# A short scan's preparation put into other steps, a convolution moved between its parts, and its drive made by GpSimd

## The chip, the cores and the metric

The kernel runs on one core of a Trainium2 chip. The metric is the device time of one execution, in microseconds. The program is one launch, and most of its instructions stand in an order that the kernel itself writes out, engine by engine.

## The reference

The input is a batch of 8 images, 64 x 64 positions of 96 channels, float32. Two layers follow each other, and each adds its result to its input:

```python
x = x + layer0(group_norm(x))
x = x + layer1(group_norm(x))
```

A layer projects 96 channels to 2 x 192 (`xp` and `z`), runs a depthwise 3x3 convolution and SiLU over `xp`, scans the result in four directions (rows, columns, and both backwards), adds the four, normalizes over channels, multiplies with silu(z) and projects back to 96. The scan of layer 0 has 16 states per channel:

```python
delta = softplus(dt @ dt_proj + bias)
h = exp(delta * A) * h + delta * B * u      # per position, 16 states
y = sum(h * C) + u * D
```

The scan of layer 1 is written with cumulative sums:

```python
dt = softplus(dt @ dt_proj_w + dt_proj_b)
decay = exp(cumsum(dt * A))
h = decay * cumsum(dt * B * u / (decay + 1e-12))
y = sum(h * C) + u * D_skip
```

Because of the term 1e-12, `h` dies away once the decay has fallen far enough, so only the beginning of each direction needs a scan at all. The kernel scans the first 160, 40, 24 and 16 positions of each direction for the four groups of four states (a constant of the kernel, with a general path for other data).

## The kernel before

Channels lie on partitions in two halves (`h`) of 96. A scan works on *sets*: 32 channels times 4 states fill 128 partitions, and a set has 1024 positions. Four sets (index `i`, 0 to 3) make a *group* of 32 channels, three groups (`g`) a *job*, which is one half of one *unit*. An image has 16 units of layer 0 (4 directions, 4 stretches), so 32 jobs and 384 sets. From the second image on, one short unit follows at the end: layer 1's scan of the image before, with 2 jobs of 3 sets of 128 x 960, 6 sets in all. Seven of the eight images have one.

The loop in `scan_rows` runs over the sets with a step number n, and each engine executes what it is given in the order of the calls. With `at(i)` as the set n + i, one step holds, in this order:

- `fetch`: SP issues the loads that spread dt and delta * u over 128 partitions (`dt_rep`, `dtu_rep`, two buffers each; for short sets also `cum_rep`). It is 5 steps ahead for ordinary groups and 2 for short sets. `replicate` and `replicate_short` load B and C (`b_rep`, `c_rep`).
- `advance_set(at(0))`: VectorE multiplies `drive` (in PSUM) with B (L895) and scans (L908). For short sets it multiplies with the gate in between (L898) and runs two scans (L903).
- `keep_state` (L919): ScalarE copies the last column, except in a direction's last stretch.
- `fill(at(1))`: ScalarE's exponential writes the decay to PSUM (L861, for short sets four pieces, L857). The pool `pslot` has two buffers.
- `drive(at(2))`, for short sets `drive(at(1))`: ScalarE copies delta * u to PSUM (L878), once a group.
- `release(at(-4))`: after a group's last set, ScalarE copies the four quarters of its sum out of PSUM (L990); for short sets `y_short` (L980).
- `gate(at(1))`: ScalarE's Tanh for a short set, four pieces (L872).
- `read_out(at(-1))`: GpSimd multiplies the scan with C (L924).
- `early(at(2))`: in the last set of a group (i = 3), GpSimd makes delta * u * B from SBUF in place of VectorE (L885), so this set has no L895.
- `collect(at(-3))`: TensorE sums over states into `acc` (L960, short sets L937). At i = 0 it first brings in what was there (L951). The pool of `acc` has one buffer.
- then the stages that stand in `plan` for this step.

Job m begins at step 12m - 1; with that as s = 0 the steps of a job are counted below. A group's `release` and the next group's first `collect` fall on s = 0, 4 and 8. In each job the stages prepare job m + 2: `ready` for an ordinary one, `short_ready` for a short one. The latter's stages are `argument` (TensorE, dt's projection), `parts`, `exponential`, `logarithm`, `rounded`, `rounding` (ScalarE: Relu and Abs, Exp, Ln, and the rounding error of 1 + exp), `total` (TensorE adds four terms, L760), `delta` (ScalarE copies the sum out, L769), `again` (TensorE, L778) and `running` (VectorE's running sum of dt, L787), `extend` (six copies on ScalarE, L505), `lowest` (eight small ScalarE instructions and two on VectorE), `product` (GpSimd, dt * u, L772) and `store` (seven memsets on GpSimd, then three DMAs on SP to DRAM). The logarithm needs its own table: ScalarE loads it and then loads the exponential's again.

All these matmuls and the convolution share one PSUM buffer (`pmisc`, tag "mm"). The convolutions for later images run beside the scan, one window a job (`conv_beside`, `windows`): 9 taps in 3 or 4 steps on TensorE (L1027), then one step for the Tanh on ScalarE (`curve`, L1037), then `product` on VectorE (L1040) and a store. Stages of the convolution stand in `plan` before those of the preparation in the same step. Jobs 30 and 31 prepare the short unit. Images 1 to 6 (counted from 0) have a convolution window in both; image 7 has none there.

Of the kernel before, what the change touches and what calls it, by code (L numbers as in the profile page):

```python
# [8 lines left out]
F32 = mybir.dt.float32  # L9
# [11 lines left out]
T = 1024  # L21
# [3 lines left out]
P = 128  # L25
# [4 lines left out]
NS = N // GS  # L30
# [23 lines left out]
def two_ss2d_layers(ctx: ExitStack, tc: tile.TileContext, t: dict, out: bass.AP):  # L54
# [368 lines left out]
    def scan_rows(xc, y, parts, plan, rows, beside):  # L423

        with (
            tc.tile_pool(name="loads", bufs=2, side="right") as loads,
            tc.tile_pool(name="piece", bufs=1) as piece,
            tc.tile_pool(name="work", bufs=2) as work,
            tc.tile_pool(name="pslot", bufs=2, space=PSUM) as pslot,
            tc.tile_pool(name="pdrive", bufs=1, space=PSUM) as pdrive,
            tc.tile_pool(name="pacc", bufs=1, space=PSUM) as pacc,  # L440
            tc.tile_pool(name="pmisc", bufs=1, space=PSUM) as pmisc,
        ):
            units, jobs, sets, x_dbl = parts
            total = len(sets)
            plan = plan(pmisc)
            with tc.manual_schedule():
                state = None
                plan.setdefault(-1, []).insert(0, lambda: low_rows(x_dbl, units[1], rows))
                for n in range(-AHEAD, max(total + 4, max(plan, default=0) + 1)):
                    at = lambda i: sets[n + i] if 0 <= n + i < total else None  # L450
                    m, j = divmod(n + 1, PER)
                    if j == 0 and 0 <= m < len(jobs):

                        stages = []
                        if m + 2 < len(jobs):
                            prepare = short_ready if jobs[m + 2]["unit"]["short"] else ready
                            stages += prepare(xc, x_dbl, jobs[m + 2], piece, pmisc)
                        if m % NH == 1 and m // NH + 2 < len(units):
                            unit = units[m // NH + 2]
                            project = short_projection if unit["short"] else projection  # L460
                            stages += project(xc, x_dbl, unit, rows, pmisc)
                        for step, stage in stages:
                            plan.setdefault(n + step, []).append(stage)
                    fetch(at(AHEAD), False, loads)
                    fetch(at(2), True, loads)
                    replicate(at(AHEAD_BC), x_dbl, loads)
                    replicate_short(at(AHEAD_BC), "b", loads)
                    replicate_short(at(AHEAD_BC - 1), "c", loads)
                    if at(0) and at(0)["unit"]["nth"] == 0 and at(0)["first"]:
                        state = piece.tile([P, D // GC * NS], F32, name="state0", bufs=2)  # L470
                    advance_set(at(0), state, work)
                    keep_state(at(-1))
                    fill(at(1), pslot)
                    drive(at(2), False, pdrive)
                    drive(at(1), True, pdrive)
                    release(at(-4), y, beside)
                    gate(at(1))
                    read_out(at(-1), work)
                    early(at(2), work)
                    collect(at(-3), xc, y, pacc)  # L480
                    for stage in plan.pop(n, []):
                        stage()
                assert not plan
# [235 lines left out]
    def short_ready(xc, x_dbl, job, piece, pmisc):  # L719
# [48 lines left out]
        def delta(s):  # L768
            nc.scalar.copy(job["ln"][:, halves[s]], job["v"])  # L769
# [17 lines left out]
            nc.vector.tensor_tensor_scan(out, ones_reset, src, 0.0, ALU.mult, ALU.add)  # L787

        def lowest():
            extend(job["cum"])  # L790
            last = small.tile([C, NS * K], F32, name="last_short")
            for i in range(NS):
                for d in range(2):
                    a, b = place(i, 2 * d), place(i, 2 * d + 1)
                    at = slice(a.start, b.start + 1, HEADS[i])
                    if d == 0:
                        at = slice(a.stop - 1, b.stop, HEADS[i])
                    nc.scalar.activation(
                        last[:, K * i + 2 * d :][:, :2],
                        job["cum"][:, at],  # L800
                        AF.Copy,
                        scale=w["least1"][:, h, i : i + 1],
                    )
            low = small.tile([C, 1], F32, name="lowest_short")
            nc.vector.tensor_reduce(low, last, mybir.AxisListType.X, ALU.min)
            nc.vector.tensor_tensor(worst, worst, low, ALU.min)

        def store():

            for i in range(NS):  # L810
                for j in (OFFSETS[i], OFFSETS[i] + HEADS[i]):
                    if j > 0:
                        nc.gpsimd.memset(job["ln"][:, j : j + BLOCK : BLOCK - 1], 1e30)
            job["dt"] = job["ln"]
            for c in ("dt", "dtu", "cum"):
                job[f"{c}_far"] = dram.tile([C, HT], F32, name=f"{c}_short", bufs=3)
                nc.sync.dma_start(job[f"{c}_far"], job[c])

# [3 lines left out]
            (1, lambda: argument(1)),  # L822
            (2, lambda: parts(1)),
            (3, exponential),
            (4, logarithm),
            (4, rounded),
            (5, rounding),
            (6, lambda: total(0)),
            (7, lambda: delta(0)),
            (7, lambda: total(1)),  # L830
            (8, lambda: delta(1)),
            (8, lambda: running(1)),
            (8, lambda: again(0)),
            (9, product),
            (9, lambda: running(0)),
            (10, lowest),
            (11, store),
        ]

    def column(s):  # L840
# [2 lines left out]

    def by_gpsimd(s):

        return s["i"] == NS - 1

    def fill(s, pslot):

# [21 lines left out]
                cum = blocks(s["group"]["cum"], i)  # L871
                nc.scalar.activation(cum, cum, AF.Tanh, bias=half_log, scale=rate)  # L872

    def drive(s, short, pdrive):

        if s and s["i"] == 0 and s["unit"]["short"] == short:
            s["group"]["drive"] = pdrive.tile([P, T], F32, name="drive")[:, : s["unit"]["n"]]
            nc.scalar.copy(s["group"]["drive"], s["group"]["dtu"])  # L878

    def early(s, work):  # L880

        if s and by_gpsimd(s):
            s["buf"] = work.tile([P, T], F32, name="set", bufs=SETS)[:, : s["unit"]["n"]]
            b = s["unit"]["b", s["i"]]
            nc.gpsimd.tensor_tensor(s["buf"], s["group"]["dtu"], b, ALU.mult)  # L885
# [202 lines left out]
    def windows(first, n, b):  # L1088
# [3 lines left out]
        for m in range(first, first + n):  # L1092
# [2 lines left out]
            projects = m % NH == 1 and (unit < K // 2 * NT or b >= 1 and unit == K * NT)  # L1095
            assert m < last
            if b >= 1 and m + NH >= K * NT * NH:
                found.append((at + 10, (3, 3, 3), 1))
            elif projects:
                found.append((at + 5, (3, 3, 3), 1))  # L1100
            else:
                found.append((at + 3, (3, 2, 2, 2), 2))
# [886 lines left out]
```

## Time and profile before

| | |
|---|---|
| time, median of 3 runs | 12404.24 us (12389.48 to 12425.54) |
| profiled execution | 12404.1 us, its span 12402.2 us |
| VectorE (DVE) busy | 10960.4 us, 88% |
| GpSimd (POOL) busy | 10508.3 us, 85% |
| ScalarE (ACT) busy | 9688.3 us, 78% |
| TensorE (PE) busy | 9540.3 us, 77% |
| mean DMA rate | 149 GB/s |
| L878, drive copy, 128x1024 | 997 ns |
| L885, delta * u * B on GpSimd, 128x1024 | 2357 ns mean |
| L924, times C on GpSimd, 128x1024 | 2359 ns mean |
| L898, gate of a short set on VectorE | 1157 to 2262 ns |

In the lines of a profile, a row of a group gives its busy time and the mean of one instruction, then the idle time of its engine just ahead of it and what ended that. In a timeline a row gives the start, the length, the engine and the line, and in brackets the idle time before it with the instruction that ended it; "x4" means that four instructions were merged. In a table of windows the columns are the length, the busy times of TensorE, its weight loads, VectorE, ScalarE and GpSimd, the granted TensorE clock, the share of the DMA engines and GB/s.

### The profile page before, as it was taken

What the parts mean: (1) busy time and instruction counts of PE and PEld (TensorE: products, weight loads), DVE (VectorE), ACT (ScalarE), POOL (GpSimd) and SP (SyncE); (2) the same over time, 40 slices, a digit from 0 to 9 for tenths busy, and PEclk for the clock granted to TensorE, in tenths of its full rate; (3) what the DMA queues carried; (4) which work ended last, traced back from release to release, by engine and by line L of the source; (5) the groups of instructions that cost most, each with busy time, mean ns of one, the idle gap of its engine ahead of it and who ended that gap; (6) DMA issues with size and microseconds to landing.
All of it is one profiled execution on the core that took longest, in us unless ns stands there. A gap on an engine that the chain in (4) does not pass through costs nothing. (4 is left out here: it accounts for less than half of the span.)

```text
span 12402.2 us, 134216 instructions
## 1 busy us (share of the span) xinstructions
PE 9540.3 (77%) x44312; PEld 3022.4 (24%) x44312; DVE 10960.4 (88%) x6870; ACT 9688.3 (78%) x15131; POOL 10508.3 (85%) x4802
## 2 busy tenths in 40 slices
PE   5875578787888778877788777888788887886565
PEld 1221122222222222222222222222222222222122
DVE  6999889996999969999799987999879998899976
ACT  4888778887887868878788787887778877788874
POOL 3999889996999969998699986999879987799974
PEclk8887778888888878888888878887788877887786
DMA  3444344444444444444444454444544445444430
GB/s 96 165 155 156 127 159 161 154 156 152 148 164 160 161 138 164 163 162 147 148 156 158 162 165 135 160 162 161 163 138 153 156 156 158 136 165 160 157 123 23
DMA packets 666561, 1853.80 MB, mean 149 GB/s; under 512 B 184936, under 2 KB 199150, under 8 KB 665757
## 3 DMA queue, kind: packets, MB, share of 16 engines
q1 hardware_dynamic: 658685, 1832.52, 44.6%
q10 hardware_dynamic: 7168, 12.59, 0.3%
q8 instruction: 352, 5.77, 0.2%
q14 instruction: 356, 2.92, 0.1%
HBM read 1533.82 MB, written 311.02 MB: 149 GB/s over the span
## 5 line engine op out<-in xcount | busy, mean ns | idle before, releaser
L924 POOL TENSOR_TENSOR out<-set,c_rep 128x1024 f32<-128x1024 f32 x3114 | 7290.0, 2359 | 884.4 <-PE acc L960 317.8
L908 DVE TENSOR_TENSOR_SCAN set<-decay,state,set 128x1024 f32<-128x1024 f32 x2304 | 5366.3, 2345 | 407.4 <-ACT decay L861 189.6
L861 ACT ACTIVATE decay<-dt_rep,w_a 128x1024 f32<-128x1024 f32 x3072 | 3420.2, 1114 | 335.7 <-DVE set L908 329.8
L895 DVE TENSOR_TENSOR set<-drive,b_rep 128x1024 f32<-128x1024 f32 x2346 | 2811.1, 1198 | 43.1 <-DMA b_rep<-x_dblr 28.2
L1027 PE MATMUL ps_conv<-edged,taps 96*96 96x512 f32 (+1 forms) x4032 | 2476.3, 754 | 54.5 <-DVE dt L787 25.9
L960 PE MATMUL acc<-out,w_gather 128*32 128x256 f32 x24576 | 2274.2, 480 | 8.1 <-POOL out L924 7.7
L908 DVE TENSOR_TENSOR_SCAN set<-decay,set 128x1024 f32<-128x1024 f32 x768 | 1744.4, 2286 | 224.5 <-ACT decay L861 146.6
L885 POOL TENSOR_TENSOR set<-dtu_rep,b_rep 128x1024 f32<-128x1024 f32 x768 | 1810.1, 2357 | 93.9 <-DMA b_rep<-x_dblr 51.6
L951 PE MATMUL acc<-map,w_eye 96*32 96x256 f32 x4608 | 568.5, 575 | 1483.4 <-ACT map L990 1253.5
L990 ACT COPY map<-acc 32x256 f32<-32x256 f32 x3072 | 1470.5, 479 | 45.8 <-PE acc L960 5.6
L960 PEld LDWEIGHTS acc<-out,w_gather 128*32 128x32 f32 x24576 | 781.8, 130 | 1939.5 <-issue 1282.0
L1027 PEld LDWEIGHTS ps_conv<-edged,taps 96*96 96x96 f32 (+1 forms) x4032 | 727.5, 200 | 1405.4 <-issue 1244.3
L919 ACT COPY state<-set 128x1 f32<-128x1 f32 x2304 | 426.1, 185 | 754.3 <-DVE set L908 747.9
L634 PE MATMUL ps_sp<-z,w_eye 96*96 96x512 f32 x960 | 658.2, 774 | 288.8 <-ACT ln L643 244.4
L655 POOL TENSOR_TENSOR dtu<-ln,map 96x1024 f32<-96x1024 f32 x256 | 670.7, 2620 | 237.2 <-DVE ln L651 133.0
L878 ACT COPY drive<-dtu_rep 128x1024 f32<-128x1024 f32 (+1 forms) x810 | 808.0, 997 | 34.7 <-DMA dtu_rep<-dtu_far 30.1
L602 PE MATMUL ps_dt<-x_dbl,w_dtw 7*96 7x512 f32 x1024 | 595.4, 663 | 301.2 <-ACT z L615 151.0
L951 PEld LDWEIGHTS acc<-map,w_eye 96*32 96x32 f32 x4608 | 101.4, 121 | 1954.6 <-ACT map L990 1656.1
L634 PE MATMUL ps_sp<-dtu,w_eye 96*96 96x512 f32 x960 | 554.6, 662 | 0.0
L634 PE MATMUL ps_sp<-ln,w_eye 96*96 96x512 f32 x960 | 535.5, 642 | 0.0
L614 ACT ACTIVATE dt<-ps_dt 96x512 f32<-96x512 f32 x512 | 303.0, 592 | 279.2 <-PE ps_dt L602 260.0
L634 PE MATMUL ps_sp<-dt,w_eye 96*96 96x512 f32 x960 | 506.7, 610 | 0.0
(239 smaller groups left out, 9496.8 us busy)
## 6 DMA issues: line engine op xcount, KB each, us to landing
dt_rep<-dt_far SPq DMA_DIRECT2D x768, 512.0 KB
dtu_rep<-dtu_far SPq DMA_DIRECT2D x768, 512.0 KB
b_rep<-x_dblr SPq DMA_DIRECT2D x256, 512.0 KB
c_rep<-x_dblr SPq DMA_DIRECT2D x256, 512.0 KB
b_rep<-x_dblc SPq DMA_DIRECT2D x256, 512.0 KB
c_rep<-x_dblc SPq DMA_DIRECT2D x256, 512.0 KB
dt_far<-ln SPq DMA_DIRECT2D x256, 384.0 KB
dtu_far<-dtu SPq DMA_DIRECT2D x256, 384.0 KB
```

Source lines behind the costliest of these rows:

```text
L634: nc.tensor.matmul(job["ps"][:C, :], w["eye"], job[term][:, halves[s]], start=i == 0, stop=i == 3,)
L655: nc.gpsimd.tensor_tensor(like(job["dtu"], col), like(job["dt"], col), positions(xc[:, h, :], col, t0, T), ALU.mult,)
L861: nc.scalar.activation(s["decay"], s["group"]["dt"], AF.Exp, scale=rate)
L878: nc.scalar.copy(s["group"]["drive"], s["group"]["dtu"])
L885: nc.gpsimd.tensor_tensor(s["buf"], s["group"]["dtu"], b, ALU.mult)
L895: nc.vector.tensor_tensor(s["buf"], s["group"]["drive"], b, ALU.mult)
L908: nc.vector.tensor_tensor_scan(ordered(s["buf"], unit), ordered(s["decay"], unit), ordered(s["buf"], unit), 0.0 if unit["nth"] == 0 else s ...
L924: nc.gpsimd.tensor_tensor(s["out"], s["buf"], s["unit"]["c", s["i"]], ALU.mult)
L951: nc.tensor.matmul(acc, lhs[:, GC * g : GC * (g + 1)], positions(old[:, h, :], unit["column"], unit["t0"] + at, n), start=True, stop=False ...
L960: nc.tensor.matmul(acc, w["gather"], s["out"][:, at : at + n], start=False, stop=s["i"] == NS - 1, skip_group_check=True,)
L990: nc.scalar.copy(yk, like(acc, unit["column"]))
L1027: nc.tensor.matmul(job["ps"][:C, :], taps[l][:k, h, tap, :], edged[:k, tap // 3 : tap // 3 + rows, tap % 3 : tap % 3 + WW], start=tap == 0 ...
```

## The change

`short_ready` keeps `argument`, `parts` and `exponential` at s = 0 to 3. `rounded` moves from 4 to 5, `logarithm` from 4 to 6, the two `total` from 6 and 7 to 8 and 9, the two `delta` from 7 and 8 to 9 and 10, `running` and `again` from 8 and 9 to 10 and 11, `product` from 9 to 11. `extend` is taken out of `lowest` and stands at 11 behind `running(0)`; `store` moves from 11 to 12, with the running sum stored first; `lowest` moves from 10 to 13. For the second short job 13 is the step of the first short set. The convolution's windows in jobs 30 and 31 begin at s = 3 in place of s = 10, so their nine taps stand at 3, 4, 5, the curve at 6, the product at 7.

For short sets, GpSimd makes delta * u * B (`by_gpsimd` is true), one step ahead and after `read_out`; the copy to PSUM and VectorE's product are left out for them.

```diff
-                    drive(at(2), False, pdrive)
-                    drive(at(1), True, pdrive)
+                    drive(at(2), pdrive)
                     release(at(-4), y, beside)
                     gate(at(1))
                     read_out(at(-1), work)
-                    early(at(2), work)
+                    early(at(2), False, work)
+                    early(at(1), True, work)
...
         def lowest():
-            extend(job["cum"])
...
-            for c in ("dt", "dtu", "cum"):
+            for c in ("cum", "dt", "dtu"):
...
             (3, exponential),
-            (4, logarithm),
-            (4, rounded),
+            (5, rounded),
             (5, rounding),
-            (6, lambda: total(0)),
-            (7, lambda: delta(0)),
-            (7, lambda: total(1)),
-            (8, lambda: delta(1)),
-            (8, lambda: running(1)),
-            (8, lambda: again(0)),
-            (9, product),
-            (9, lambda: running(0)),
-            (10, lowest),
-            (11, store),
+            (6, logarithm),
+            (8, lambda: total(0)),
+            (9, lambda: delta(0)),
+            (9, lambda: total(1)),
+            (10, lambda: delta(1)),
+            (10, lambda: running(1)),
+            (10, lambda: again(0)),
+            (11, product),
+            (11, lambda: running(0)),
+            (11, lambda: extend(job["cum"])),
+            (12, store),
+            (13, lowest),
         ]
...
     def by_gpsimd(s):
-        return s["i"] == NS - 1
+        return s["unit"]["short"] or s["i"] == NS - 1
...
-    def drive(s, short, pdrive):
-        if s and s["i"] == 0 and s["unit"]["short"] == short:
-            s["group"]["drive"] = pdrive.tile([P, T], F32, name="drive")[:, : s["unit"]["n"]]
+    def drive(s, pdrive):
+        if s and s["i"] == 0 and not s["unit"]["short"]:
+            s["group"]["drive"] = pdrive.tile([P, T], F32, name="drive")
             nc.scalar.copy(s["group"]["drive"], s["group"]["dtu"])
-    def early(s, work):
-        if s and by_gpsimd(s):
+    def early(s, short, work):
+        if s and by_gpsimd(s) and s["unit"]["short"] == short:
...
             if b >= 1 and m + NH >= K * NT * NH:
-                found.append((at + 10, (3, 3, 3), 1))
+                found.append((at + 3, (3, 3, 3), 1))
```

## The prediction

> **What bounds the kernel now.** First the page's busy times and costliest groups.
>
> ```profile
> PE 9540.3 (77%) x44312; PEld 3022.4 (24%) x44312; DVE 10960.4 (88%) x6870; ACT 9688.3 (78%) x15131; POOL 10508.3 (85%) x4802
> L924 POOL TENSOR_TENSOR out<-set,c_rep 128x1024 f32<-128x1024 f32 x3114 | 7290.0, 2359 | 884.4 <-PE acc L960 317.8
> L908 DVE TENSOR_TENSOR_SCAN set<-decay,state,set 128x1024 f32<-128x1024 f32 x2304 | 5366.3, 2345 | 407.4 <-ACT decay L861 189.6
> ```
>
> VectorE sets the pace: three sets in four cost it a product and a scan, 3.56 us from scan end to scan end in the timeline, the fourth a scan alone, 2.3. Where it idles it mostly waits for ScalarE's decays (L861). ScalarE can't run far ahead: `pslot` has two buffers, so the decay of set s+1 starts when scan s-1 has ended. That leaves it 3.56 us a step for 1.1 us of decay and all else.
>
> Then the stretch that the change touches: two jobs of 12 sets (from the end of scan 359 to the end of scan 383), by the windows view, the last four columns being ScalarE, GpSimd, clock and DMA.
>
> ```profile
> 4307.13:4402.06 94.93, 67.57 (x317) 20.42 (x315) 80.71 (x51) 71.02 (x112) 77.80 (x49) 0.77 0.53 157
> 5816.07:5914.87 98.80, 72.20 (x319) 22.13 (x317) 80.73 (x52) 70.64 (x112) 77.93 (x49) 0.74 0.52 150
> 7324.75:7422.77 98.02, 70.59 (x319) 21.64 (x317) 80.71 (x51) 70.59 (x112) 77.86 (x49) 0.75 0.51 151
> 8832.49:8929.78 97.29, 69.67 (x318) 21.46 (x316) 80.82 (x51) 70.75 (x112) 77.90 (x49) 0.75 0.52 152
> 11845.46:11936.85 91.39, 48.12 (x286) 14.97 (x284) 80.01 (x50) 69.64 (x110) 77.83 (x48) 0.72 0.39 128
> ```
>
> These are images 2 to 5 and 7 (7 has no convolution there). With images 1 and 6 (93.6 and 94.9, each lacking one scan's record, so 3.5 longer) the mean of 1 to 6 is 97.4, of which VectorE idles 16.7. VectorE's timeline of image 1 tells on what:
>
> ```profile
> 2820.95 2.35 DVE L908 TENSOR_TENSOR_SCAN set<-decay,state,set 128x1024 f32<-128x1024 f32 x1 [1.95 <-ACT decay L861]
> 2830.96 0.82 DVE L787 TENSOR_TENSOR_SCAN dt<-ones_reset,ps_sp 96x320 f32<-96x320 f32 x1 [1.85 <-ACT ln L769]
> 2855.06 0.68 DVE L1040 SCALAR_TENSOR_TENSOR conv_out<-conv_out,ps_conv 96x512 f32<-96x512 f32 x1 [2.07 <-ACT conv_out L1037]
> 2873.25 2.35 DVE L908 TENSOR_TENSOR_SCAN set<-decay,state,set 128x1024 f32<-128x1024 f32 x1 [3.83 <-ACT decay L861]
> 2903.32 1.16 DVE L898 SCALAR_TENSOR_TENSOR set<-cum_rep,set 128x960 f32<-128x960 f32 x1 [3.31 <-ACT cum_rep L872]
> ```
>
> In order: the logarithm's two table loads beside a release (step 4); the second `delta` behind a release (step 8); the convolution's curve; step 4 again; the first gate of the short unit.
>
> One more view, TensorE's and ScalarE's timelines of an ordinary convolution in image 3, carries the forecast.
>
> ```profile
> 5706.59 1.08 PE L951 MATMUL acc<-map,w_eye 96*32 96x256 f32 x8 [4.14 <-ACT map L990]
> 5708.46 3.23 PE L1027 MATMUL ps_conv<-edged,taps 96*96 96x512 f32 x4
> 5712.19 1.96 PE L1027 MATMUL ps_conv<-edged,taps 96*96 96x512 f32 x4
> 5714.65 1.96 PE L1027 MATMUL ps_conv<-edged,taps 96*96 96x512 f32 x4
> ```
> ```profile
> 5704.14 2.40 ACT L990 COPY map<-acc 32x256 f32<-32x256 f32 x4
> 5716.64 0.59 ACT L1037 ACTIVATE conv_out<-ps_conv 96x512 f32<-96x512 f32 x1
> ```
>
> `acc` has one buffer, so at steps 0, 4, 8 of a job TensorE's first `collect` of a group (L951) waits for ScalarE's `release` (L990) of that same step, and all that is queued behind it waits too. Six taps behind the release end 10.0 us after it. Over the 124 such windows that stand whole in the trace, L951 to the last tap takes 7.9 to 14.9, mean 10.7. ScalarE reaches the curve just then only because the logarithm (step 6) stands ahead of it (step 7).
>
> **Two rules of the Trainium skill.** "SBUF — State Buffer", Who interferes with whom: a VectorE instruction with two SBUF inputs contends with a GpSimd one that reads SBUF. Here L898 takes 1.16 alone and up to 2.26 beside GpSimd; its product with the PSUM `drive` stays at 1.13. GpSimd will now always be busy, so I take 2.2 for L898; the trace decides. "TensorE: Matmul & The Clock Gate", What's actually happening: after an idle window of about 3.4 us the clock is halved. Above, four matmuls take 3.23 after 4.14 idle and 1.96 later; the forecast goes by these rows.
>
> **The short unit** (42 sets, 6 in each of images 1 to 7). Removed: the `drive` copy (0.94, ScalarE) and the product (1.13, VectorE) of each. Added: 42 GpSimd products. No 128x960 form of L885 is in the trace; bounds are L772 (96x960, 2.23) and L885 (128x1024, 2.36); I take 2.25. GpSimd then has 4.5 a set (with L924, 2.22), VectorE 4.4 (2.2 and two scans 2.2); before, VectorE's steps were about 5.6. What eats the gain: `extend` (0.9, ScalarE), now at step 11, waits for `running(0)` at the end of VectorE's step and pushes the first gate back by what the missing copy gave; `lowest` (1.6 on ScalarE, 0.6 on VectorE) of the second job now falls into the second short set, where VectorE waits 1.4 for it; the release behind the fourth set still costs 2.4. Laid end to end: the first L898 5.0 us after scan 383 (before 5.1), the others at 11.1, 15.5, 20.0, 26.3, 30.7, the last scan's end 35.1 (before 36.7 in every image). The six collects, each waiting for `y_short`, end 41.1 (before about 42.7). Gain 1.5 per image.
>
> Queues: SP's store of the second job moves a step later, behind a fetch that it held up before; it now waits for a memset behind GpSimd's first product, and the next fetch waits behind it. That fetch is issued some 6 us ahead of its use. GpSimd's product waits for its own `dtu_rep` at step -1, `read_out` queued behind it. All these covers hold by 3 to 6 us; without them see the second rival.
>
> **The preparation and the convolution, images 1 to 6.** Zero is the end of scan 3; scans 4 to 7 end at 2.3, 5.9, 9.4, 13.0. ScalarE: decay and release end at 3.6. TensorE: six taps behind that release (3+3 instead of 2+2+2, one collect of 0.6 fewer, so 10.1) end at 13.7. The curve now stands at step 6, *ahead* of the logarithm. ScalarE has done the roundings (2.0) and decay 7 by 7.8 and waits till 13.8; curve 0.6, table load, Ln, table load 3.6, decay 8: 19.0. Scan 8 was due at 13.0: 6.0 late (the convolution's product, 0.7, lies inside). Copy 1.0, decay 9 1.1, release 2.4: 23.5. Now `total(0)` at step 8 stands behind L951: L951 and L960 1.7, four terms 4.2 (3.5 to 5 in the trace, by clock): 29.4; `delta(0)` 0.55, `total(1)` 3.6, `delta(1)` 0.55: 34.2. VectorE ends scan 10 at 28.4 and waits for that `delta(1)` in `running(1)`: 5.9 late. Then 0.8, a set, 0.75, scan 12 at 41.7; without waits 30.5. The same sum for the kernel before gives 2.0 and 1.9 where the timeline has 1.95 and 1.85.
>
> Two jobs: 10.7 + 41.7, then 10.7 + 0.6 (`lowest`) + 41.7, 105.3, and 0.5 for small waits on GpSimd: 105.8 against 97.4, **+8.4**; with the short unit +6.9, six images **+41**. Gone is the old step-4 stall, the curve's wait behind the next job's argument, and the convolution in the short unit (which had cover: 36.7 with it and without). Behind the late scan only GpSimd's `read_out` queues, which idles as long. The input load of the last chunk moves 7 steps ahead, to the place that it has in other jobs: nothing. Image 7 (no convolution): the logarithm just fits, `running(1)` is 5.0 late twice; 91.6 + 0.5 against 91.4, less 1.5: -1.
>
> The profiled execution took 12404.1 (span 12402.2 and 1.9 around it), the median is 12404.24: **12444**. What a measurement can tell from no change is 0.3%, 37 us: the line is 12441, so the likeliest case sits on it.
>
> **Rivals.**
> 1. *It ends faster.* The taps are through when ScalarE comes to the curve, and the sums aren't held by the release. Then two jobs take the 80.3 us of a good ordinary pair (images 2 and 5, the two jobs before: 80.2 and 80.4) plus 4.4 for the short unit's own scans, 84.7: -12.7 in six images, -6.7 in the seventh, and -1.5 seven times: -93, **12311**. For it: the preparation leaves the release's steps 4 and 8. Against: it needs six taps within 4.2 us of a release, and the shortest in the trace take 7.9. Half of it (one of the two waits much smaller, 5 us less a job): -60 on the forecast, 12384.
> 2. *The transfers become the bound.* In image 1 DMA is at 0.96 and 356 GB/s from 2900 to 2910, in the short unit. If a fetch lands 2 us late for each of five sets: 10 an image, seven images, +70: **12514**. Against: VectorE, ScalarE wait for none there now.
> 3. *The clock stays low.* Six taps at 14.9 rather than 10.7, in all 12 windows: +50, **12494**. For it: the convolutions in this stretch have 4.0 to 5.3 us per three taps, mostly slow.
> 4. *The steps don't shift anything* (each queue absorbs them): 12404. Against: the waits are in the instruction order.
>
> **Numbers.** Main case 0.53 (spread by the clock and the sums' cold start, 12410 to 12480); rival 1 full 0.08, half 0.16; rival 2 0.08; rival 3 0.11; rival 4 0.04. Slower: 0.65 of the main case (small waits add up more than they cancel), rivals 2 and 3: 0.54. Same: the rest of it, rival 4 and 0.10 of the half rival 1: 0.32. Faster: full rival 1 and 0.06 of its half: 0.14. Range 12375 to 12505, which leaves out full rival 1 and rival 2's end; the likeliest case's own is 12410 to 12480.
>
> **What would show it.** Right: L1037 in these jobs idles about 6 us for PE; L787 idles 5 to 6 for ACT ln (2.5 before); the stretch of two jobs is near 106 in images 1 to 6 and 92 in image 7; the short unit's last scan ends 35 after scan 383; L878 and L895 lose 42. Wrong: L787 without idle, the stretch under 95, or GpSimd L885 waiting for `dtu_rep` in the short unit.

## The result and the profile after

The changed kernel takes **12468.69 us** (median of 10 runs, 12453.65 to 12501.59) against 12405.51 for the kernel before, run beside it (10 runs): ratio 1.0053, 95% interval 1.0041 to 1.0064. It is slower by 66 us, inside the forecast range and 25 us above the forecast time. The profiled execution has a span of 12479.0 us (12402.2 before).

The page's busy times and the costliest VectorE group, the scan, have hardly moved:

```profile
PE 9520.4 (76%) x44312; PEld 3021.3 (24%) x44312; DVE 10937.2 (88%) x6828; ACT 9653.5 (77%) x15089; POOL 10621.4 (85%) x4844
L908 DVE TENSOR_TENSOR_SCAN set<-decay,state,set 128x1024 f32<-128x1024 f32 x2304 | 5367.2, 2345 | 412.6 <-ACT decay L861 187.3
```

VectorE has 42 instructions fewer and GpSimd 42 more, as the change says. GpSimd is 113 us busier, 106 of them the new products in the short units; no other engine is busier than before. So the loss is either those products or waiting. The windows view of the same two jobs shows waiting (from the end of scan 359 to the end of scan 383; an image's ordinary scans are counted from 0, so 383 is the last one). Images 2 to 5 and 7:

```profile
4320.22:4429.21 108.99, 72.97 (x324) 22.41 (x322) 82.33 (x51) 68.12 (x102) 78.37 (x42) 0.72 0.47 147
5849.81:5959.33 109.52, 73.55 (x324) 22.29 (x322) 82.31 (x50) 67.77 (x102) 78.31 (x42) 0.73 0.46 145
7381.02:7491.93 110.91, 75.55 (x326) 22.83 (x324) 82.44 (x50) 67.69 (x102) 78.36 (x42) 0.73 0.46 142
8902.83:9010.88 108.05, 72.14 (x324) 21.91 (x322) 82.36 (x51) 67.78 (x102) 78.37 (x42) 0.74 0.46 146
11916.16:12014.52 98.36, 52.76 (x289) 16.62 (x287) 80.75 (x48) 67.03 (x100) 78.43 (x42) 0.67 0.40 128
```

With images 1 and 6 (110.5 and 107.3) the mean of 1 to 6 is 109.2, 11.8 above before. VectorE's busy time in it is 82.3 (80.7 before), its idle time 26.9 (16.7 before). VectorE's timeline of image 2 shows on what, in the second job and the first short sets:

```profile
4405.81 2.35 DVE L908 TENSOR_TENSOR_SCAN set<-decay,state,set 128x1024 f32<-128x1024 f32 x1 [4.13 <-ACT decay L861]
...
4421.95 0.82 DVE L787 TENSOR_TENSOR_SCAN dt<-ones_reset,ps_sp 96x320 f32<-96x320 f32 x1 [6.65 <-ACT ln L769]
...
4434.31 2.37 DVE L898 SCALAR_TENSOR_TENSOR set<-cum_rep,set 128x960 f32<-128x960 f32 x1 [5.10 <-POOL out L924]
```

The 4.13 is the scan behind curve and logarithm, the 6.65 the running sum behind the sums. ScalarE's timeline of the same stretch:

```profile
4400.36 0.59 ACT L1037 ACTIVATE conv_out<-ps_conv 96x512 f32<-96x512 f32 x1 [5.03 <-PE ps_conv L1027]
4400.98 1.28 ACT L755 ACT_TABLE_LOAD   x1
4402.27 1.00 ACT L755 ACTIVATE ln<-z 96x960 f32<-96x960 f32 x1
4403.29 1.28 ACT L861 ACT_TABLE_LOAD   x1
4404.59 1.12 ACT L861 ACTIVATE decay<-dt_rep,w_a 128x1024 f32<-128x1024 f32 x1
...
4407.63 2.40 ACT L990 COPY map<-acc 32x256 f32<-32x256 f32 x4
...
4417.25 0.56 ACT L769 COPY ln<-ps_sp 96x480 f32<-96x480 f32 x1 [6.33 <-PE ps_sp L760]
```

ScalarE stands 5.0 us at the curve for the taps, then runs the whole logarithm, and only then the decay; later it stands 6.3 us at `delta(0)` for the sums. TensorE's timeline says why those came late:

```profile
4410.07 1.08 PE L951 MATMUL acc<-map,w_eye 96*32 96x256 f32 x8 [8.74 <-ACT map L990]
...
4411.94 1.92 PE L760 MATMUL ps_sp<-z,w_eye 96*96 96x480 f32 x2
4413.65 1.81 PE L760 MATMUL ps_sp<-dtu,w_eye 96*96 96x480 f32 x2
4415.25 1.16 PE L760 MATMUL ps_sp<-ln,w_eye 96*96 96x480 f32 x2
4416.25 0.97 PE L760 MATMUL ps_sp<-dt,w_eye 96*96 96x480 f32 x2
...
4417.86 1.05 PE L760 MATMUL ps_sp<-z,w_eye 96*96 96x480 f32 x2
```

The first sum starts behind L951, which waited for the release and starts 0.04 us after L990's end (4407.63 + 2.40 = 4410.03). And TensorE comes out of 8.7 us of idling slow: the same product of z takes 1.92 the first time and 1.05 six microseconds later. The windows view of TensorE alone, cut where its granted clock changes, shows the same. The columns are the length, TensorE's busy time, the granted clock, the DMA share and GB/s; half the clock is granted until 5.6 us after work has resumed at 4410.07:

```profile
4405.39:4415.63 10.24, 5.56 (x21) 0.50 0.83 208
4415.63:4425.87 10.24, 7.80 (x38) 1.00 0.39 130
```

### Where the time went, for all kernels

Three lengths of a profiled execution account for nearly all of the timed differences: the two jobs in images 1 to 6 (mean), the two jobs in image 7, and what follows scan 383 up to the first centring of the next stage (L1606), summed over seven images, which holds the short unit. "By trace" is their sum, six times the first included, less that of before; "by ratio" is the timed ratio, as microseconds on 12405. All 384 scans of each image are in each trace; images 1 and 6 of before, which the forecast has shorter by a scan, take 97.2 and 98.4.

| kernel | two jobs, 1 to 6 | image 7 | after scan 383, seven | by trace | by ratio | ratio, 95% |
|---|---|---|---|---|---|---|
| before | 97.4 | 91.4 | 307.5 | | | |
| after | 109.2 | 98.4 | 296.6 | +67 | +66 | 1.0053, 1.0041 to 1.0064 |
| e1 GpSimd part alone | 97.6 | 91.4 | 292.5 | -14 | -26 | 0.9979, 0.9967 to 0.9990 |
| e2 steps alone | 110.1 | 96.0 | 325.3 | +99 | +96 | 1.0077, 1.0055 to 1.0098 |
| e3 curve behind logarithm | 98.1 | 96.0 | 299.6 | 0 | +1 | 1.0001, 0.9991 to 1.0012 |
| e4 sums a step later | 103.5 | 88.7 | 291.1 | +17 | +12 | 1.0010, 1.0002 to 1.0018 |
| e5 both | 93.4 | 90.0 | 287.5 | -45 | -43 | 0.9965, 0.9951 to 0.9980 |
| e6 twelve warm products | 107.9 | 93.8 | 302.1 | +60 | +55 | 1.0044, 1.0027 to 1.0061 |
| e7 gate in PSUM | 108.3 | 98.5 | 298.0 | +62 | +79 | 1.0064, 1.0049 to 1.0080 |
| e8 e5 with gate in PSUM | 93.4 | 91.8 | 286.3 | -45 | -41 | 0.9967, 0.9957 to 0.9977 |
| e9 nine warm products | 103.5 | 92.5 | 296.8 | +26 | +32 | 1.0026, 1.0014 to 1.0038 |
| e12 one-input minimum | 109.0 | 97.2 | 298.9 | +66 | +77 | 1.0062, 1.0040 to 1.0084 |
| e13 e5 and one-input minimum | 87.9 | 85.9 | 284.1 | -86 | -74 | 0.9940, 0.9916 to 0.9964 |

Each sum by trace lies within the interval of its ratio. So these two stretches are the place to read a variant's cause from.

### The profile page after: what moved, and what is told of

It is laid out like the page before. It is cut to its first block, busy times and chain, and to the rows that moved or that the text cites. A ratio compares the mean times of both kernels' runs of the same rounds, so it can differ in the third digit from the quotient of the medians.

```text
span 12479.0 us, 134118 instructions
## 1 busy us (share of the span) xinstructions
PE 9520.4 (76%) x44312; PEld 3021.3 (24%) x44312; DVE 10937.2 (88%) x6828; ACT 9653.5 (77%) x15089; POOL 10621.4 (85%) x4844
## 5 line engine op out<-in xcount | busy, mean ns | idle before, releaser
L924 POOL TENSOR_TENSOR out<-set,c_rep 128x1024 f32<-128x1024 f32 x3114 | 7305.2, 2365 | 786.3 <-DVE set L908 326.7
L895 DVE TENSOR_TENSOR set<-drive,b_rep 128x1024 f32<-128x1024 f32 x2304 | 2762.5, 1199 | 43.7 <-DMA b_rep<-x_dblr 43.7
L1027 PE MATMUL ps_conv<-edged,taps 96*96 96x512 f32 (+1 forms) x4032 | 2450.7, 747 | 29.7 <-ACT z L615 25.4
L885 POOL TENSOR_TENSOR set<-dtu_rep,b_rep 128x1024 f32<-128x1024 f32 (+1 forms) x810 | 1917.9, 2368 | 101.8 <-DMA b_rep<-x_dblr 43.8
L951 PE MATMUL acc<-map,w_eye 96*32 96x256 f32 x4608 | 570.7, 577 | 1589.1 <-ACT map L990 1349.8
L990 ACT COPY map<-acc 32x256 f32<-32x256 f32 x3072 | 1472.2, 479 | 46.3 <-PE acc L960 6.0
L878 ACT COPY drive<-dtu_rep 128x1024 f32<-128x1024 f32 x768 | 768.2, 1000 | 36.8 <-DMA dtu_rep<-dtu_far 29.9
L951 PEld LDWEIGHTS acc<-map,w_eye 96*32 96x32 f32 x4608 | 102.0, 122 | 2062.3 <-ACT map L990 1754.2
```

The lines of the kernel that those rows point to most:

```text
L895: nc.vector.tensor_tensor(s["buf"], s["group"]["drive"], b, ALU.mult)
L924: nc.gpsimd.tensor_tensor(s["out"], s["buf"], s["unit"]["c", s["i"]], ALU.mult)
L951: nc.tensor.matmul(acc, lhs[:, GC * g : GC * (g + 1)], positions(old[:, h, :], unit["column"], unit["t0"] + at, n), start=True, stop=False ...
L990: nc.scalar.copy(yk, like(acc, unit["column"]))
L1027: nc.tensor.matmul(job["ps"][:C, :], taps[l][:k, h, tap, :], edged[:k, tap // 3 : tap // 3 + rows, tap % 3 : tap % 3 + WW], start=tap == 0 ...
```

## The experiments

The theory: the steps cost some 40 us or more by two waits, the curve ahead of the logarithm (a) and the sums behind the release (b), and the GpSimd part gains a little. The rivals: the GpSimd part or its transfers cost the time; or TensorE's clock does, wherever the work stands.

### The two halves of the change

`e1_gpsimd_only` is the kernel before with `by_gpsimd`, `drive` and `early` of the change; `e2_steps_only` is the changed kernel with these three as before.

```diff
 # e1, on the kernel before; e2 undoes this on the changed one
-        return s["i"] == NS - 1
+        return s["unit"]["short"] or s["i"] == NS - 1
...
-                    drive(at(1), True, pdrive)
...
+                    early(at(1), True, work)
```

> The kernel before with only the GpSimd part of the change: GpSimd makes delta * u * B of the short sets, no drive copy, no product on VectorE; preparation and convolution in their old steps. My theory (the loss lies in two waits of the preparation, on the convolution's curve and on the sums): the two jobs of preparation stay at 97.4 us in images 1 to 6, the short unit stays at 36 to 37 us because GpSimd and VectorE block one another, time 12395 to 12415. Rival (GpSimd's product is what costs, by lying in front of read_out): short unit 40 us or more, time 12435 or more. Rival (the product is worth what its 1.1 us on VectorE suggest): short unit 31 to 33, time 12370.

> The kernel after with the GpSimd part undone: the short sets get their drive copy and VectorE's product again; preparation and convolution in the new steps. My theory: two jobs stay near 109 us in images 1 to 6 and 98 in image 7, the short unit is 37 to 39 (extend and lowest now delay it and the copy is back), time 12465 to 12480. Rival (GpSimd's product costs): back to within 15 us of the kernel before, 12420 or less.

Measured: 12380.32 and 12497.13 against 12411.99. Both missed their ranges, on opposite sides: the GpSimd part gains 26 us, the steps cost 96. So the rival that GpSimd's products cost the time falls. Within their intervals they add up: after against e2 the difference is 30 us by the ratios, and 296.6 - 325.3 = -28.7 us of it stand in the stretch after scan 383. In the short unit's last scan nothing seems to happen (36.8 us after scan 383 in after, 36.7 before), but two moves cancel there: the new steps alone put it to 39.5 (e2), and the GpSimd part takes 2.7 off again. With the old steps it takes 1.0 off in the mean (e1: 33.9 to 36.8). The rest of the gain is in what ScalarE does there. Its timelines of before (first fence, scan 383 ends at 4402.06) and of e1 (second, 4385.86):

```profile
4431.37 0.94 ACT L878 COPY drive<-dtu_rep 128x960 f32<-128x960 f32 x1
4432.33 0.30 ACT L980 ACTIVATE y_short<-acc 128x160 f32<-128x160 f32 x1
...
4443.61 0.30 ACT L980 ACTIVATE y_short<-acc 128x160 f32<-128x160 f32 x1 [1.91 <-PE acc L937]
```
```profile
4414.36 0.30 ACT L980 ACTIVATE y_short<-acc 128x160 f32<-128x160 f32 x1
...
4425.62 0.30 ACT L980 ACTIVATE y_short<-acc 128x160 f32<-128x160 f32 x1 [1.91 <-PE acc L937]
```

The six collects and their `y_short` copies go back and forth between TensorE and ScalarE, 2.2 us a turn, and end the unit. In before the first copy stands behind a drive copy, 30.3 us after scan 383; in e1 it comes at 28.5, and the last one moves from 41.6 to 39.8. In this image of e1 the last scan came 1.9 earlier too; the two parts of the gain were not separated. The forecast's second rival is seen here in small: GpSimd's L885 idles 13.9 us in all for `dtu_rep` in e1; in after it idles 0.0.

### The curve behind the logarithm

```diff
-                found.append((at + 3, (3, 3, 3), 1))
+                found.append((at + 3, (3, 3, 3, 0), 0))
```

An empty step after the taps puts the curve to step 7 and leaves the product at 7.

> The kernel after with one thing moved: in jobs 30 and 31 the convolution's curve stands one step later, at 7, behind the logarithm at 6; its product stays at 7. My theory: ScalarE does the logarithm while TensorE finishes the taps, the 4.1 us that VectorE waits for the decay go, some 1.5 us remain at the product; 4 to 5 us less a job in images 1 to 6, none in image 7; the wait of L787 for the sums stays at 5.7 or more. Time 12410 to 12425. Rival (the convolution costs by holding up TensorE's collects and the shared PSUM buffer, not by its curve's place on ScalarE): time 12455 or more.

Measured 12417.92, ratio 1.0001: the curve's place is worth 65 us (1.0053 to 1.0001). The window of image 2, and ScalarE's timeline:

```profile
4288.38:4388.54 100.16, 76.18 (x326) 23.21 (x324) 82.26 (x51) 67.55 (x102) 78.50 (x42) 0.72 0.50 156
```
```profile
4358.71 1.28 ACT L755 ACT_TABLE_LOAD   x1
...
4365.22 0.59 ACT L1037 ACTIVATE conv_out<-ps_conv 96x512 f32<-96x512 f32 x1 [0.85 <-PE ps_conv L1027]
```

The logarithm now fills the time in which the taps run, ScalarE's wait at the curve falls from 5.0 to 0.85 and the decay's 4.1 is gone from all six images. The sums profit too; TensorE idles 3.0 to 5.1 us ahead of them in these images in place of 8.7, and L787's waits are 4.2 to 5.4, mean 4.9, in place of 6.9. The two jobs are 67 us shorter than in after, six images together; of these some 43 are wait (a) itself (the decay and the product wait 4.6 us a job in after, 1.1 in e3) and 24 lie at L787. The rival, that the convolution costs by holding up the collects and the PSUM buffer, falls.

### The sums a step away from the release

```diff
-            (8, lambda: total(0)),
-            (9, lambda: delta(0)),
-            (9, lambda: total(1)),
-            (10, lambda: delta(1)),
-            (10, lambda: running(1)),
-            (10, lambda: again(0)),
-            (11, product),
-            (11, lambda: running(0)),
-            (11, lambda: extend(job["cum"])),
-            (12, store),
+            (9, lambda: total(0)),
+            (10, lambda: delta(0)),
+            (10, lambda: total(1)),
+            (11, lambda: delta(1)),
+            (11, lambda: running(1)),
+            (11, lambda: again(0)),
+            (12, product),
+            (12, lambda: running(0)),
+            (12, lambda: extend(job["cum"])),
+            (13, store),
```

> The kernel after with one thing moved: total, delta, running, again, product and extend of the short preparation one step later (sums at 9 and 10, running at 11 and 12, store and lowest at 13). My theory: the sums start when they did, right behind the release on TensorE, but what VectorE and ScalarE ask of them is due a set later; L787 waits 2 to 4 us for ACT ln in place of 5.7 to 9.7, in all 14 jobs, image 7 too: 40 to 55 us less, 12414 to 12429. Rival (the sums are late because the late curve pushes them, so a step more changes nothing, or the store that comes later holds up the fetches of the short unit): 12455 or more, or a short unit of 39 us or more.

Measured 12418.21, ratio 1.0010: the sums' place is worth 53 us by the ratios, 49 by trace, of which 44 lie at L787. It idles 2.2 to 5.2 (8.5 once), and the decay's 4.1 stays. Then both edits at once, with the nine taps as 3, 2, 2, 2 so that the curve stands at 7 and the product at 8:

```diff
-                found.append((at + 3, (3, 3, 3), 1))
+                found.append((at + 3, (3, 2, 2, 2), 1))
```

> The kernel after with both waits eased: sums one step later (as in the run before of that name) and the convolution in the ordinary pattern of 3, 2, 2, 2 taps from step 3, so that its curve is at 7, behind the logarithm, and its product at 8. My theory: the two effects add up, as they sit at different places of the same chain; two jobs at 88 to 93 us in images 1 to 6, L787 waits under 3 us, no decay waits of 4 us; time 12355 to 12385, 20 to 50 us below the kernel before. Rival (TensorE's last taps or the shared PSUM buffer take what is gained: curve, product and sums now follow each other at 7, 8, 9): the sums wait for the product instead, 12400 or more.

Measured **12358.51**, ratio 0.9965 (0.9951 to 0.9980): faster than both kernels. The two edits alone gave 65 and 53; together it is 109. The waits are not as small as expected: L787 idles 3.2 in the mean and up to 5.3, and the two jobs take 93.4. Its window of image 2, where VectorE idles 12 of 94 us:

```profile
4298.58:4393.00 94.42, 75.49 (x325) 22.05 (x323) 82.05 (x51) 68.71 (x100) 78.75 (x42) 0.73 0.53 166
```

### The clock in the sums

The forecast had L787 idle 5.9; after has 5.7 to 9.7, mean 6.9 in images 1 to 6. Is the rest the slow clock? `e6_warm` gives TensorE something to do: twelve products whose result nobody reads, in step 7.

```diff
+        def warm():
+            job["v"] = bank(0, "ps_warm")
+            for _ in range(12):
+                nc.tensor.matmul(job["v"], w["eye"], job["z"][:, halves[0]], start=True, stop=True)
...
+            (7, warm),
             (8, lambda: total(0)),
```

> The kernel after with 12 extra matmuls on TensorE at step 7 of the short preparation (the transposing weights times z, into the shared PSUM buffer, never read), which fill the idle time ahead of the release. My theory for the size that I missed (the first sum took 5.8 us in place of 4.2 because TensorE had idled 8.7 us and ran at half clock): the first four terms take 3.6 to 4.2 us, L787 waits 1.5 to 2.5 us less a job, 14 jobs: 12435 to 12450. Rival (the terms are slow for another reason, such as operands or the weight loads): no change, or a few us slower from the extra work.

Measured 12453.57, above its range: 11 us below after by the ratios, which their intervals can't tell apart. The sums did run fast (3.5 us in all 14 jobs), but the timeline shows a fault of the experiment: in image 2 the twelve products took 9.9 us and held L951 up for 1.4 us after the release had ended. So nine instead of twelve (`range(9)`):

> The changed kernel with nine unused products instead of twelve at s = 7 (the twelve ended 1.4 us after the release and held up the first collect themselves). If the sums were late because TensorE ran them at half clock after its idle window, then the first sum now starts with the release's end and takes 3.5 us as the second does: the waits of L787 fall from a mean of 7 to about 4.5 us in jobs where the products end before the release, two jobs take 105 to 107 us in place of 109.2, and the kernel 12430 to 12445. If the wait is the release's place alone, L787 stays near 5.9 as with twelve products, and the time near 12453.

Measured 12441.92, ratio 1.0026, its interval just clear of after's. TensorE's timeline of image 2 in e9 (a few lines are added above this code: L959 is L951, L998 is L990, L794 is L787), and VectorE's:

```profile
4389.99 7.49 PE L771 MATMUL ps_warm<-z,w_eye 96*96 96x480 f32 x18 [0.40 <-DVE conv_out L1048]
4398.36 1.05 PE L959 MATMUL acc<-map,w_eye 96*32 96x256 f32 x8 [0.89 <-ACT map L998]
...
4399.77 1.05 PE L760 MATMUL ps_sp<-z,w_eye 96*96 96x480 f32 x2
4400.65 0.97 PE L760 MATMUL ps_sp<-dtu,w_eye 96*96 96x480 f32 x2
```
```profile
4407.96 0.82 DVE L794 TENSOR_TENSOR_SCAN dt<-ones_reset,ps_sp 96x320 f32<-96x320 f32 x1 [4.41 <-ACT ln L776]
```

L794 idles 4.40 to 4.44 in eleven of the twelve jobs (6.7 in the other). Of the mean wait of 6.9, then, 4.4 are the release's place and 2.5 the clock; fourteen times that is 35 us, and the ratios differ by 33. In after the wait follows the clock job by job: where the first sum takes 4.3 to 4.4 us (granted clock 0.78 to 0.80 in it), L787 waits 5.5 to 5.7; where it takes 6.7 (clock 0.50), and the second sum is slow too, it waits 9.3 to 9.7. Two jobs came down further than expected, to 103.5, because the waits behind the curve were 0.6 us a job shorter too.

### The gate in PSUM

In the short unit the mean L898 went from 1767 ns to 2013, and GpSimd got slower too. Two timelines of image 2 of after, VectorE and GpSimd:

```profile
4441.20 1.14 DVE L898 SCALAR_TENSOR_TENSOR set<-cum_rep,set 128x960 f32<-128x960 f32 x1
...
4449.91 3.16 DVE L898 SCALAR_TENSOR_TENSOR set<-cum_rep,set 128x960 f32<-128x960 f32 x1 [2.04 <-POOL set L885]
```
```profile
4441.22 3.20 POOL L885 TENSOR_TENSOR set<-dtu_rep,b_rep 128x960 f32<-128x960 f32 x1
...
4449.83 2.23 POOL L924 TENSOR_TENSOR out<-set,c_rep 128x960 f32<-128x960 f32 x1
```

Who starts first runs at its own length, and the other one ends that much later: L885 starts 0.02 behind an L898 of 1.14 and takes 3.20 where 2.21 is its own time; L898 starts 0.08 behind an L924 of 2.23 and takes 3.16, which is 2.0 more. `e7_gate_psum` takes one of L898's two SBUF inputs away, by having ScalarE write the Tanh to the PSUM buffer that the drive no longer needs.

```diff
+            s["gate"] = pdrive.tile([P, T], F32, name="drive")[:, : s["unit"]["n"]]
...
-                nc.scalar.activation(cum, cum, AF.Tanh, bias=half_log, scale=rate)
+                nc.scalar.activation(blocks(s["gate"], i), cum, AF.Tanh, bias=half_log, scale=rate)
...
-                buf, s["group"]["cum"], 1.0, buf, ALU.add, ALU.mult
+                buf, s["gate"], 1.0, buf, ALU.add, ALU.mult
```

> The kernel after with the short sets' gate (ScalarE's Tanh) written to the PSUM buffer of drive, which short sets no longer use, in place of SBUF; so VectorE's L898 has one SBUF input and not two. My theory for the missing gain of the short unit (L898 and GpSimd's two products exclude one another: 2.2 + 2.2 + 1.15 = 5.6 us a set whatever else is moved): L898 takes 1.2 us throughout, GpSimd's products 2.2, the short unit ends 31 to 33 us after the last ordinary scan in place of 36.8; 12430 to 12450. Rival (the unit is bound by the transfers, at 0.96 of DMA, or by ScalarE's six-us steps): 36 us or more, 12460 or more.

Groups of after, then of e7:

```profile
L898 DVE SCALAR_TENSOR_TENSOR set<-cum_rep,set 128x960 f32<-128x960 f32 x42 | 84.5, 2013 | 64.3 <-POOL out L924 35.8 <-POOL set L885 28.6
L885 POOL TENSOR_TENSOR set<-dtu_rep,b_rep 128x960 f32<-128x960 f32 x42 | 106.4, 2533 | 0.0
L924 POOL TENSOR_TENSOR out<-set,c_rep 128x960 f32<-128x960 f32 x42 | 103.7, 2469 | 51.8 <-DVE set L903 28.1 <-issue 20.3 <-DMA dtu_rep<-dtu_short 3.4
```
```profile
L898 DVE SCALAR_TENSOR_TENSOR set<-drive,set 128x960 f32<-128x960 f32 x42 | 48.5, 1155 | 71.3 <-ACT drive L870 65.6 <-POOL set L885 5.7
L885 POOL TENSOR_TENSOR set<-dtu_rep,b_rep 128x960 f32<-128x960 f32 x42 | 93.2, 2218 | 0.7 <-DMA dtu_rep<-dtu_short 0.7
L924 POOL TENSOR_TENSOR out<-set,c_rep 128x960 f32<-128x960 f32 x42 | 93.1, 2216 | 60.4 <-DVE set L903 42.5 <-issue 15.7 <-PE acc L937 2.2
```

All three means fall to their own lengths, and each of the 42 L898 lies between 1.142 and 1.159: the exclusion is shown. The time does not follow: 12467.07, ratio 1.0064, a clear miss. The last scan ends 34.7 in the mean after scan 383 instead of 36.8, but L898 now idles 65.6 us for the gate itself (its PSUM pool has one buffer; a second was not tried), and the turns of `y_short` after it end no sooner: 298.0 in the table, 296.6 in after. `e8_all` put the same edit on e5, with `lowest` of the second job at step 19:

> All of it together: both waits eased, the gate in PSUM, and the second short job's lowest at step 19, behind the short unit, so that VectorE doesn't wait for it in the second short set. My theory: the unit ends 29 to 32 us after the last ordinary scan, two jobs at 88 to 93 us, time 12310 to 12350, faster than the kernel before and than the GpSimd part alone (12380). Rival (the unit then becomes bound by its fetches): unit 34 or more, L885 or ScalarE's decay waiting for the loads, 12360 or more.

Measured 12369.32, ratio 0.9967, no different from e5: a second miss, with the last scan at 33.5 and L898 waiting 87.0 us for the gate. The rival shows as well, GpSimd's L885 waiting 8.9 us for loads.

### The minimum with one input

Two rows of the groups of after go beyond the 0.6 us of VectorE that the forecast gave to `lowest`, which ends with a product of two SBUF columns, L805, 96x1. Before (there it is L806) it took 452 ns in the median and the reduction ahead of it waited for nobody; now:

```profile
L805 DVE TENSOR_TENSOR worst<-worst,lowest_short 96x1 f32<-96x1 f32 x14 | 22.7, 1620 | 0.5
L804 DVE TENSOR_REDUCE lowest_short<-last_short 96x1 f32<-96x16 f32 x14 | 2.3, 166 | 12.5 <-ACT last_short L797 12.5
```

One element a partition, and 1.62 us: it waits until GpSimd's product ends. VectorE and GpSimd in image 2 of after, then of before:

```profile
4439.74 1.53 DVE L805 TENSOR_TENSOR worst<-worst,lowest_short 96x1 f32<-96x1 f32 x1
4439.05 2.21 POOL L924 TENSOR_TENSOR out<-set,c_rep 128x960 f32<-128x960 f32 x1 [3.39 <-issue]
```
```profile
4395.84 0.46 DVE L806 TENSOR_TENSOR worst<-worst,lowest_short 96x1 f32<-96x1 f32 x1
4393.94 2.34 POOL L885 TENSOR_TENSOR set<-dtu_rep,b_rep 128x1024 f32<-128x1024 f32 x1
```

In both, VectorE's product ends within 0.02 us of GpSimd's. So the 0.45 of before was a wait as well, only a shorter one. Where GpSimd stands idle, in the second job of e2, the same product takes 0.15 to 0.16.

`e12_lowest_one_input` on the changed kernel and `e13_both_one_input` on e5 make one reduction of it:

```diff
-            last = small.tile([C, NS * K], F32, name="last_short")
+            last = small.tile([C, NS * K + 1], F32, name="last_short")
+            nc.scalar.copy(last[:, NS * K :], worst)
...
-            low = small.tile([C, 1], F32, name="lowest_short")
-            nc.vector.tensor_reduce(low, last, mybir.AxisListType.X, ALU.min)
-            nc.vector.tensor_tensor(worst, worst, low, ALU.min)
+            nc.vector.tensor_reduce(worst, last, mybir.AxisListType.X, ALU.min)
```

> The changed kernel, with the minimum of `lowest` taken without VectorE's product of two SBUF tiles (L805): ScalarE copies the running minimum into the tile that the reduction reads, 0.2 us more for it, and one reduction of 17 columns writes it back. If L805 took 1.62 us in place of 0.45 because it waited for GpSimd's L924 to end, then it is gone: two jobs lose 1.6 to 1.8 us less 0.2 (one `lowest` lies in them), the short unit's VectorE another 1.5, and the kernel takes 12445 to 12458 where 12469 was measured. If the 1.62 lies beside other waits anyway (the reduction's own wait for ScalarE grows, or the next product waits for GpSimd as long), nothing changes: 12462 to 12475.

> The same in the kernel with both later sums and shared convolution steps (12358.5, L805 1.78 us there): 12330 to 12350 if L805's waiting is on VectorE's path, 12355 to 12365 if it is covered.

e13 took **12325.39**, ratio 0.9940: the lowest median of all, below its range, 0.6% under the kernel before; its interval (0.9916 to 0.9964) still overlaps that of e5. By trace the two jobs fell by 5.5 us: 2.3 are L805 itself (its length in those two jobs of e5), 1.8 in the mean are curve waits that e13 does not have (4.1 in images 2 and 3, 1.4 in 4 and 6), and 0.7 lie at L787. Why the curve waits went with it was not tested. e12 shows no gain as a time: 12471.39 lies in the range named for no effect, and its ratio, 1.0062, can't be told from after's. Its trace has five images at a mean of 107.6, the 1.6 below 109.2 that was expected, and one, image 6, at 115.9, where L787 idled 11.4 twice. TensorE's timeline there, and its window until the clock returns:

```profile
10399.53 1.08 PE L950 MATMUL acc<-map,w_eye 96*32 96x256 f32 x8 [8.75 <-ACT map L989]
...
10412.36 1.80 PE L760 MATMUL ps_sp<-ln,w_eye 96*96 96x480 f32 x2
```
```profile
10394.77:10415.25 20.48, 15.72 (x40) 0.50 0.19 62
```

After the same 8.7 us of idling the slow clock stayed through both sums, 15.7 us of work. e2 has 11.4 twice as well. So wait (b) is 5.7 in one image of these kernels and 11.4 in another, and a kernel that lets TensorE idle there can carry that in its spread.

## Why the prediction was right, point by point

Both waits stand where the forecast put them, and each shrank when it alone was moved (e3, e4). The sizes were off: the total was short by 26 us, with `lowest` and the sums too small and the curve too large.

- **The curve ahead of the logarithm.** Forecast: the curve waits about 6 us for the taps, and scan 8 is 6.0 us late, the product of 0.7 inside. Measured: the curve waits 3.6 to 6.5, mean 5.3, and the decay and the convolution's product wait 4.6 us a job in the mean (2.5 to 6.2), 5.3 with the product. The step is right, and e3 shows that the order of these two on ScalarE is the cause. The size was 0.7 too large: from L951 to the last tap it took 9.3 us in the mean, not 10.1.
- **The sums behind the release.** Forecast 5.9; measured mean 6.9, up to 9.7; image 7, forecast 5.0 twice, has 9.3 and 5.5. The place was right (e4). The term that was mis-sized is the four products of `total(0)`: I took 4.2 us "by clock" for the first sum; it took 4.3 to 6.7, mean 5.3, behind 8.7 us of idling that the forecast itself creates, while warm it takes 3.5 (e9). The earlier timeline had shown the slow clock after 4.1 us of idling; I named it for the spread and left all but 0.7 us of it out of the sum. The Trainium skill, "TensorE: Matmul & The Clock Gate", What's actually happening, has the halving after an idle window of some 3.4 us and full speed again after a busy one. The traces agree with the halving: in image 2 TensorE stops at 4401.3, and the granted clock falls at 4405.39. The return there, 5.6 us after work resumed, still fits a window of 3.4 us that does not start with the work; the 15.7 us of image 6 of e12 do not.
- **`lowest`.** Forecast 0.6 in the two jobs and a wait of 1.4 in the short unit. Measured: a wait of 1.2 in the two jobs and 0.6 in the unit, and 1.7 and 1.5 for L805, which had been 0.45. Mis-sized because I took the 0.45 as the length of VectorE's small product; it was already a wait for GpSimd, and how long that wait is depends on where in GpSimd's product it begins.
- **Two jobs.** Forecast 105.8 (+8.4), measured 109.2 (+11.8). Of the 3.4 more, the L787 waits give 2.0 and `lowest` 2.4, small waits for GpSimd some 0.5, and the curve gives 1.4 less. Image 7: 92.1 forecast, 98.4 measured, 4.8 more at L787 and 2.4 at `lowest`.
- **The short unit.** Forecast a last scan at 35.1 and 1.5 us gained an image; measured 36.8, and 1.6 gained (10.9 in seven). That the gain came out right is luck. I had L898 at 2.2 and GpSimd's two at 2.25 and 2.22, since L924 had shown no stretching before (2.21 to 2.24 in the short units); they are 2.0, 2.5 and 2.5, because the exclusion works both ways: the sixth gate starts at 31.4 where 30.7 was forecast, and takes 3.16 itself. The Trainium skill, "SBUF — State Buffer", Who interferes with whom, says that the shared port pair is an exclusive lock and that the order of issue decides who blocks; the rows above agree, and the forecast should have gone by that for GpSimd too. What was gained instead is the drive copies' place on ScalarE: the first `y_short` comes at 28.1 (before 29.8 to 30.4), and the last one at 41.0 in six of the seven images, 4.2 behind the last scan.
- **The rivals.** The faster case fell: its two conditions, taps through and sums free of the release, were eased only by moving the steps again (e3, e4, e5), and then the kernel was faster than before. The transfers showed in e1 and e8, with 13.9 and 8.9 us of GpSimd's time in seven images; in after L924 waits 3.4 us for them. The low clock was real, in the sums and not in the taps, where I had looked for it: 7.6 to 10.4 us from L951 to the last tap, where that rival had 14.9.
- **The total.** +40 forecast, +66 measured by the ratio. By trace, of the 26 us more, L787 gives 17, `lowest` 17 and small waits some 3, and the curve gives 8 less. All of the slow clock at the sums costs 33 (e9); some 10 of these were in the forecast.

## What to carry to other kernels

Where one PSUM buffer ties a matmul to another engine's release, cost what is queued behind it from the end of the release, and at the clock that the wait itself leaves behind; the same matmuls were worth 3.5, 5.3 or 6.7 us. When work must wait for TensorE on a busy in-order engine, put the longest independent piece ahead of it (here the logarithm ahead of the curve: 65 us of 12400 for the order of two instructions). And before VectorE and GpSimd are put side by side, look for VectorE's instructions with two SBUF inputs, down to the 96x1 ones, and ask of each length in a trace whether it is already a wait.

## What the runs showed of the hardware that was not expected

- VectorE and GpSimd shut each other out in both directions: with two SBUF inputs on VectorE, L898 went from 1.14 to 3.16 and L885 from 2.21 to 3.20, and a 96x1 product that takes 0.15 beside an idle GpSimd took up to 1.71 in after and 2.35 in e5. With one of L898's inputs in PSUM, L898 and GpSimd's two products were back at their own lengths (1.155, 2.218 and 2.216).
- After 8.7 us of idling TensorE was granted half its clock for the first 5.6 us of work in one image and for 15.7 in another, at the same instructions.
- Nine unused products on an idle TensorE made the changed kernel 0.27% faster (1.0053 to 1.0026).
